# Cross-attention on one core: scalings and weight sums leave VectorE, and the order of sums, moves and steps is set anew

## The chip, the cores and the metric

One Trainium2 chip, one of its cores. The metric is the device time of one execution of the kernel in microseconds, as the median of three runs; beside it one execution was recorded by the profiler. A core has TensorE (matrix products; PE in the profile, its weight loads PEld), VectorE (DVE), ScalarE (ACT), GpSimd (POOL) and SyncE (SP), which here issues nearly all DMA transfers. Each engine works off its own queue of instructions in the order in which the program emits them.

## The reference

All data are float32. There are 8 batch elements of 256 rows and 1024 columns, 32 heads of 32 columns, and 256 context rows per batch element, which serve as keys and as values.

```
mu, var = mean(x), var(x)                       # over the 1024 columns
h = (x - mu) * rsqrt(var + 1e-5) * gamma + beta
Q = split_heads(h @ Wq.T);  K = V = split_heads(ctx)
scores = Q @ K.T / sqrt(32);  scores = where(mask, scores, -inf)
attn = softmax(scores) @ V
out = x + merge_heads(attn) @ Wout.T
```

## The kernel before, in words

**Units of work.** A quad is four heads of one batch element (128 of the 1024 columns), so there are 8 quads for each of the 8 batch elements, 64 in all, numbered from 0. The main loop (line 1006) has one iteration, called slot n below, for each quad. In slot n TensorE computes the scores of quad n+1 (`scores`, line 477), then the values product of quad n-2 (`values`, line 632), and between them and behind them steps of the output projection of an earlier batch element (`product_steps`, line 712) and a part of the query projection of a later one (`make_q`, line 335, or `query_product`, line 436). The other engines do the softmax of quad n+1 (`softmax_parts`, line 505). A block b is the output projection of batch element b; it lies in slots 8(b+1) to 8(b+1)+8, which are counted i = 0 to 8 within the block.

**Softmax of a quad.** For each head j of four and each half s of the 256 rows, VectorE adds the mask and takes the row minimum (line 529), ScalarE takes the exponential and its row sum (line 533). `normalize` (line 538) takes the reciprocal on VectorE and then scales the head's two 128x256 tiles: on GpSimd, unless the table `SCALED_BY` (lines 497 to 503) names ScalarE (A, line 544) or VectorE (V, line 546). This pair of instructions is called a scaling of a quad's head. Then VectorE transposes the head's blocks of 32x32 into `pT` (line 552), ScalarE copies half of that aside to `pc` (line 558), and after the fourth head SP moves pieces between partitions (lines 618 and 622), so that the values product can read them. The score banks in PSUM are four, one for each head: the scores of quad n+2 can only be written once VectorE has read those of quad n+1.

**Projections by Strassen's scheme.** From batch element 2 on the query projection is made of seven products of 512-blocks instead of eight, and so is the output projection of every block (the tables `Q_PRODUCTS` and `PRODUCTS`). That needs sums of weight blocks, made once (`sum_wo` line 177, `sum_wq` line 389; the tables `WO_SUMS` and `WQ_SUMS`, lines 876 to 882, give slot, sum, chunk and engine), and sums of activations for each batch element (`sum_at`, `sum_x`), on GpSimd. The weights' sums for the query are kept in DRAM (`KEEPS`) and come back through the tile `ring`.

**Output steps.** Each block has 28 steps (seven products, four chunks each; a step shows as two instructions in the profile). The tables `FIRST_STEPS` (block 0), `ASIDE_STEPS` (blocks 2 to 5) and `STEPS` (block 1) give, for each slot i of the block, how many steps stand at three places: behind the scores, behind the values product, and behind all the rest of the slot. The bank in which a product accumulates is emptied by VectorE, or ScalarE, at slots fixed in lines 994 to 999 (`take`, `store`, `keep_p1`); what begins in the same bank waits for that.

**Layer norm of a later batch element.** `loads` brings x, `stats` takes mean and variance on VectorE, `norms` normalizes (`ln_norm`, line 245, on ScalarE unless the table `NORM_BY`, line 496, or the call says otherwise), `trans` transposes blocks on VectorE, and `moves` moves 16 pieces between partitions by DMAs on SP (line 331). The slots of these five are given in lines 829 to 858, for batch element 3 and later as distances to the first slot in which the new x is used. Each of them also stands in the order of its engine's queue at that slot.

**Folds.** For batch element 0 the query weights are used as they come; for the later ones each of the 8 chunks is scaled by gamma once (`fold`, line 363), on the engine given by `FOLDED_BY` and at the slots in the list in lines 908 and 935.

**SP's queue.** In each slot SP issues the values of a later quad (line 144), the two moves of line 618, then the loads of the slot (keys, x, residuals, weights of the output projection by `WO_LOADS`, line 210, whose third entry is the slot, or below 0 for the start), the two moves of line 622, and then the moves of x.

Of the kernel before, what the change touches and what calls it, by code (L numbers as in the profile page):

```python
# [59 lines left out]
def xattn_kernel(  # L60
# [149 lines left out]
    WO_LOADS = [[3, 0, -1], [2, 0, 0], [3, 1, -2], [0, 0, 3], [2, 1, -1], [0, 1, -1]]  # L210
# [284 lines left out]
    FOLDED_BY = 'PPVPPPPP'  # L495
    NORM_BY = {(2, 0): nc.vector, (2, 1): nc.gpsimd}
    SCALED_BY = {}
    ENGINES = {"P": nc.gpsimd, "A": nc.scalar, "V": nc.vector}
    for q, j, e in [[63, 2, 'A'], [18, 0, 'V'], [17, 2, 'A'], [16, 2, 'A'], [15, 3, 'A'], [15, 2, 'A'], [15, 0, 'A'],
# [3 lines left out]
        SCALED_BY[q, j] = ENGINES[e]  # L503
# [143 lines left out]
    def copy_at(n):  # L647
# [4 lines left out]
        for r, pv in enumerate(pvs.pop(n)):  # L652
# [22 lines left out]
    FIRST_STEPS = ((0, 0, 0), (0, 4, 2), (0, 2, 3), (0, 1, 1), (0, 3, 1),  # L675
                   (0, 2, 1), (0, 0, 3), (0, 1, 1), (0, 3, 0))
    ASIDE_STEPS = ((0, 0, 0), (0, 6, 0), (0, 2, 0), (0, 4, 0), (0, 4, 2),
                   (0, 0, 1), (0, 1, 4), (0, 0, 0), (0, 4, 0))
# [147 lines left out]
    for b in range(1, B):  # L826
# [3 lines left out]
        elif b == 2:  # L830
            when = dict(
                **{'loads': [0, 1],
         'moves': [5, 5, 5, 5, 5, 5, 6, 6, 6, 6, 6, 7, 7, 7, 7, 7],
         'norms': [3, 3],
# [3 lines left out]
        else:  # L838
            REL = dict(loads=(-13, -12), stats=(-11, -9), norms=(-8, -7), trans=(-7, -6),
                       moves=[-6 + (i + 2) // 6 for i in range(16)])  # L840
            if b == 3:
                REL.update(loads=(-12, -11), stats=(-10, -9))
                REL.update({'loads': [-13, -11],
         'moves': [-6, -6, -5, -5, -5, -5, -5, -5, -5, -4, -4, -4, -4, -3, -3, -3],
         'norms': [-8, -7],
         'stats': [-10, -9],
         'trans': [-6, -6]})
            else:
                REL.update({'loads': [-13, -12],
         'moves': [-6, -6, -6, -6, -6, -6, -6, -5, -5, -5, -4, -4, -4, -4, -4, -4],  # L850
         'norms': [-9, -7],
# [19 lines left out]
        if b % 2 == 0:  # L871
# [351 lines left out]
```

## Time and profile before

| | us |
|---|---|
| median of 3 runs | 583.51 (583.2 to 586.84) |
| profiled execution | 583.09 |
| its span, first to last instruction | 581.3 |
| busy in the span: TensorE / weight loads | 566.2 / 396.1 |
| VectorE / ScalarE / GpSimd | 476.7 / 422.7 / 395.1 |

The share of busy time is not the share of necessary time: matrix instructions are pipelined, and their ends are modelled, so a TensorE that is shown as busy may still be waiting in part. A row of a group reads: line, engine, operation, output and inputs by the program's names, shapes, count, then busy time and the mean time of one, then the idle time of the engine just before them and what ended it. In rows in order of time the first number is the start from the beginning of the span and the second the length; "x2" says that neighbouring instructions are merged. The letters f32 after a shape are the type.

### The profile page before, as it was taken

The numbers are of one execution on the slowest core, as the hardware profiler recorded it, in microseconds if no ns is written. First come the engines' busy times: TensorE is split into PE (matmuls) and PEld (weight loads), VectorE is DVE, ScalarE is ACT, GpSimd is POOL, SyncE is SP. The second block draws the span as 40 slices with busy tenths as digits, with TensorE's granted clock in tenths as the row PEclk, the third lists the DMA queues.
The fourth block names the chain that finished last, engine by engine and source line by source line (L and its number), as shares of the span: only waits on it lengthen the run. The fifth ranks groups of instructions, "written<-read, shape, count | busy, mean of one in ns | idle before, by whom it ended". The sixth has DMA issues, their size and how long they took to land.

```text
span 581.3 us, 20175 instructions
## 1 busy us (share of the span) xinstructions
PE 566.2 (97%) x7258; PEld 396.1 (68%) x7258; DVE 476.7 (82%) x1717; ACT 422.7 (73%) x1465; POOL 395.1 (68%) x628
## 2 busy tenths in 40 slices
PE   8999999799899999999999999999999999999997
PEld 7788885476666776676776777767776777755443
DVE  5999989899897888988889877988978769779823
ACT  4597987678887976787677876788767767769920
POOL 2689996769748665875748866686657667358780
PEclk9999999899999999999999999999999999999999
DMA  8965877657768778887778777777667876446651
GB/s 306 368 173 157 236 202 203 223 172 236 203 198 247 202 193 242 229 223 197 221 209 248 223 214 203 233 220 213 203 160 205 230 198 182 140 133 182 202 164 72
DMA packets 48051, 120.07 MB, mean 207 GB/s; under 512 B 9168, under 2 KB 9936, under 8 KB 47952
## 3 DMA queue, kind: packets, MB, share of 16 engines
q1 hardware_dynamic: 47664, 118.79, 70.4%
q8 instruction: 57, 0.93, 0.7%
q14 instruction: 42, 0.34, 0.2%
q10 hardware_dynamic: 288, 0.01, 0.0%
HBM read 67.38 MB, written 11.53 MB: 136 GB/s over the span
## 4 chain that ended last, share of the span: by engine, by line
PE 66%; DVE 7%; ACT 5%; DMA 2%; issue 1%; POOL 1%; SPq 0%; DVEq 0%
PE po_S L730 16%; PE pq_A L446 16%; PE pv L640 8%; PE sc L485 8%; PE po_A L730 8%; PE pq_S L446 6%; ACT e L533 3%; PE po_end L797 2%; DVE e L529 2%; DVE pT L552 2%; DVE e L546 1%; PE po_last L797 1%; ACT e L544 1%; DMA pT<-pT 1%; POOL e L546 1%
## 5 line engine op out<-in xcount | busy, mean ns | idle before, releaser
L546 POOL TENSOR_SCALAR e<-e,rden 128x256 f32<-128x256 f32 x464 | 215.3, 482 | 135.1 <-DVE rden L540 132.9
L533 ACT ACTIVATE e<-e,mn 128x256 f32<-128x256 f32 x512 | 254.0, 501 | 45.2 <-DVE mn L529 43.5
L552 DVE STREAM_TRANSPOSE pT<-e 128x512 f32<-128x512 f32 x256 | 180.4, 706 | 44.2 <-POOL e L546 33.3
L529 DVE CUSTOM_DVE_ANT_0 e<-sc,mb 128x256 f32<-128x256 f32 x512 | 185.1, 415 | 18.8 <-PE sc L485 18.4
L558 ACT COPY pc<-pT 128x512 f32<-128x512 f32 x128 | 79.0, 617 | 69.9 <-DVE pT L552 40.0
L533 ACT ACTIVATION_READ_ACCUMULATOR e<-e,mn 128x1 f32 x512 | 98.1, 192 | 0.0
L485 PE MATMUL sc<-k,qa 32*128 32x256 f32 x1024 | 74.7, 401 | 1.6 <-DVE qa L467 0.9
L640 PE MATMUL pv<-pT,v 64*32 64x128 f32 x4096 | 74.7, 274 | 0.9 <-DMA pT<-pT 0.8
L730 PE MATMUL po_S<-wo,at 128*128 128x512 f32 x152 | 73.1, 607 | 1.3 <-DVE r L772 0.7
L640 PEld LDWEIGHTS pv<-pT,v 64*32 64x32 f32 x4096 | 57.3, 105 | 24.2 <-issue 15.1
L485 PEld LDWEIGHTS sc<-k,qa 32*128 32x128 f32 x1024 | 46.5, 184 | 36.8 <-issue 13.4
L730 PE MATMUL po_A<-wo,at 128*128 128x512 f32 x128 | 59.6, 606 | 0.2 <-ACT p L738 0.2
L344 PE MATMUL pq<-xnT,wq 128*128 128x256 f32 (+1 forms) x240 | 55.0, 384 | 0.0
L730 PE MATMUL po_S<-wo,s 128*128 128x512 f32 x104 | 50.2, 620 | 3.9 <-DVE r L772 3.5
L446 PEld LDWEIGHTS pq_A<-xnT,wq 128*128 128x128 f32 x416 | 48.2, 192 | 5.1 <-issue 3.9
L344 PEld LDWEIGHTS pq<-xnT,wq 128*128 128x128 f32 x240 | 44.6, 190 | 8.2 <-issue 1.7
L446 PE MATMUL pq_A<-xnT,wq 128*128 128x128 f32 x416 | 49.0, 276 | 0.0
L730 PEld LDWEIGHTS po_S<-wo,at 128*128 128x128 f32 x152 | 26.1, 190 | 25.0 <-issue 22.6
L529 DVE DVE_READ_ACCUMULATOR2_ANT mn<- 128x1 f32 x512 | 42.3, 83 | 0.0
L730 PEld LDWEIGHTS po_A<-wo,at 128*128 128x128 f32 x128 | 22.8, 189 | 25.8 <-issue 24.4
L540 DVE RECIPROCAL rden<-den 128x2 f32<-128x2 f32 x256 | 37.6, 147 | 2.5 <-ACT e L533 1.7
L730 PEld LDWEIGHTS po_S<-wo,s 128*128 128x128 f32 x104 | 19.0, 196 | 23.7 <-issue 19.1
(99 smaller groups left out, 689.1 us busy)
## 6 DMA issues: line engine op xcount, KB each, us to landing
v<-in_kv_dram SPq DMA_DIRECT2D x32, 512.0 KB, 5.1
pT<-pT SPq DMA_DIRECT2D x128, 128.0 KB, 2.6
pT<-pc SPq DMA_DIRECT2D x128, 128.0 KB, 3.8
ring<-kept_T SPq DMA_DIRECT2D x22, 512.0 KB, 5.9
k<-in_kv_dram SPq DMA_DIRECT2D x32, 256.0 KB, 3.8
x<-in_x_dram SPq DMA_DIRECT2D x14, 512.0 KB, 5.1
r<-in_x_dram SPq DMA_DIRECT2D x28, 256.0 KB, 4.7
out_dram<-r SPq DMA_DIRECT2D x28, 256.0 KB, 2.7
```

The costliest lines, as they stand in the source:

```text
L344: nc.tensor.matmul(pqs[n], wq[:, o, c, :], xnTs[b](c), start=(c == 0), stop=(c == NC - 1),)
L446: nc.tensor.matmul(pqs[b][:, o, :], w[:, c], x_[:, c], start=begins and o + c == 0, stop=c == NK - 1, skip_group_check=True,)
L485: nc.tensor.matmul(scs[n][j][:, s, :], qa[r, n % NQ, ts(s, P)], ks[n - n % 2][r, n % 2, :], start=True, stop=True,)
L529: nc.vector.tensor_tensor_reduce(out=e[:, s, :], in0=pss[j][:, s, :], in1=mbs[n // NQ], scale=1.0, scalar=NO_SCORE, op0=ALU.add, op1=ALU.m ...
L533: nc.scalar.activation(e[:, s, :], e[:, s, :], AF.Exp, bias=mn[:, s : s + 1], scale=-1.0, accum_out=den[:, s : s + 1],)
L540: nc.vector.reciprocal(rden, dens[j])
L546: engine.tensor_scalar(es[j][:, s, :], es[j][:, s, :], rden[:, s : s + 1], 1.0, ALU.mult, ALU.mult,)
L552: nc.vector.transpose(pT[:, :, :, j, :, :].rearrange("p a i s k -> p (a i) s k"), es[j].rearrange("p s (b t) -> p b s t", t=K),)
L558: nc.scalar.copy(pc[:, :, ts(j, 2)], pT[:, 1, :, ts(j, 2)])
L640: nc.tensor.matmul(pvs[n][r][j * HD : (j + 1) * HD], vs[n - n % 2][ts(r, 2 * K), n % 2, i, ts(j, HD)], pT[ts(r, 2 * K), :, i, j, :, :], st ...
L730: nc.tensor.matmul(po, operand(b, name)[:, c], wo[:, which, c], start=begins and c == 0, stop=c == NK - 1, skip_group_check=not begins,)
L797: nc.tensor.matmul(po, end_operand(name)[:, c], wo[:, which, c, cols], start=c in begins, stop=True, skip_group_check=True,)
```

## The change

It alters tables and two engine assignments; no computation is added or left out.

- Scaling: the seven pairs on VectorE (quads 1, 5, 10 twice, 12 twice, 18) go to GpSimd or ScalarE. ScalarE scales 20 pairs, all in quads 3 to 16, instead of 17; in quad 10 these are heads 0, 1 and 2. GpSimd scales 236 pairs instead of 232.
- Weight sums: the three query sums on VectorE go to GpSimd, and the slots of many sums are new.
- Folds: all on GpSimd, at new slots (two before slot 0 instead of one).
- Normalization: the second half of batch element 1 goes from GpSimd to VectorE, the second half of element 2 from GpSimd to ScalarE.
- Output steps of block 0 and blocks 2 to 5 are spread over their slots in another way; the same 28 for each.
- Loads, moves, norms and transpositions of batch elements 2 and later are at other slots in part, and so are some loads of output weights and the keeping of sums. In the diff the first table with `moves` is that of batch element 2, the second that of element 3, the third that of elements 4 to 7.

```diff
-    WO_LOADS = [[3, 0, -1], [2, 0, 0], [3, 1, -2], [0, 0, 3], [2, 1, -1], [0, 1, -1]]
+    WO_LOADS = [[3, 0, -1], [0, 0, 3], [0, 1, 1], [3, 1, -1], [2, 0, 2], [2, 1, 2]]
...
-    FOLDED_BY = 'PPVPPPPP'
-    NORM_BY = {(2, 0): nc.vector, (2, 1): nc.gpsimd}
+    FOLDED_BY = 'PPPPPPPP'
+    NORM_BY = {(2, 0): nc.vector}
...
-    for q, j, e in [[63, 2, 'A'], [18, 0, 'V'], [17, 2, 'A'], [16, 2, 'A'], [15, 3, 'A'], [15, 2, 'A'], [15, 0, 'A'],
-         [14, 3, 'A'], [13, 3, 'A'], [12, 3, 'V'], [12, 2, 'A'], [12, 1, 'V'], [11, 3, 'A'], [11, 2, 'A'],
-         [10, 3, 'V'], [10, 0, 'V'], [9, 3, 'A'], [8, 3, 'A'], [6, 3, 'A'], [6, 2, 'A'], [5, 3, 'A'],
-         [5, 2, 'A'], [5, 0, 'V'], [1, 0, 'V']]:
+    for q, j, e in [[3, 3, 'A'], [4, 3, 'A'], [5, 3, 'A'], [6, 2, 'A'], [6, 3, 'A'], [8, 3, 'A'], [10, 0, 'A'],
+         [10, 1, 'A'], [10, 2, 'A'], [11, 1, 'A'], [11, 2, 'A'], [11, 3, 'A'], [12, 2, 'A'], [13, 2, 'A'],
+         [13, 3, 'A'], [14, 3, 'A'], [15, 0, 'A'], [15, 2, 'A'], [15, 3, 'A'], [16, 2, 'A']]:
...
-    FIRST_STEPS = ((0, 0, 0), (0, 4, 2), (0, 2, 3), (0, 1, 1), (0, 3, 1),
-                   (0, 2, 1), (0, 0, 3), (0, 1, 1), (0, 3, 0))
-    ASIDE_STEPS = ((0, 0, 0), (0, 6, 0), (0, 2, 0), (0, 4, 0), (0, 4, 2),
-                   (0, 0, 1), (0, 1, 4), (0, 0, 0), (0, 4, 0))
+    FIRST_STEPS = ((0, 0, 0), (0, 5, 0), (0, 3, 0), (0, 4, 3), (0, 1, 0),
+                   (0, 3, 0), (0, 1, 3), (0, 1, 1), (0, 3, 0))
+    ASIDE_STEPS = ((0, 0, 0), (0, 4, 4), (0, 0, 4), (0, 0, 1), (0, 3, 1),
+                   (0, 0, 0), (0, 3, 4), (0, 0, 0), (0, 4, 0))
...
-                **{'loads': [0, 1],
-         'moves': [5, 5, 5, 5, 5, 5, 6, 6, 6, 6, 6, 7, 7, 7, 7, 7],
-         'norms': [3, 3],
+                **{'loads': [0, 0],
+         'moves': [5, 5, 5, 5, 5, 6, 6, 6, 6, 6, 6, 6, 7, 7, 7, 7],
+         'norms': [2, 3],
...
-                REL.update({'loads': [-13, -11],
-         'moves': [-6, -6, -5, -5, -5, -5, -5, -5, -5, -4, -4, -4, -4, -3, -3, -3],
-         'norms': [-8, -7],
+                REL.update({'loads': [-13, -10],
+         'moves': [-6, -6, -6, -6, -5, -5, -5, -5, -4, -4, -4, -4, -4, -4, -4, -4],
+         'norms': [-9, -7],
          'stats': [-10, -9],
-         'trans': [-6, -6]})
+         'trans': [-7, -6]})
...
-         'moves': [-6, -6, -6, -6, -6, -6, -6, -5, -5, -5, -4, -4, -4, -4, -4, -4],
-         'norms': [-9, -7],
+         'moves': [-6, -6, -6, -6, -6, -6, -6, -5, -5, -4, -4, -4, -4, -4, -4, -4],
+         'norms': [-9, -8],
...
-    WO_SUMS = [[6, 4, 1, 'P'], [2, 5, 1, 'P'], [5, 4, 0, 'P'], [3, 5, 0, 'P'], [5, 5, 2, 'P'], [11, 6, 1, 'P'],
-         [13, 3, 1, 'P'], [6, 5, 3, 'P'], [11, 6, 2, 'P'], [9, 4, 2, 'P'], [12, 6, 3, 'P'], [11, 6, 0, 'P'],
-         [10, 4, 3, 'P'], [14, 3, 3, 'P'], [13, 3, 0, 'P'], [12, 3, 2, 'P']]
-    WQ_SUMS = [[11, 'T2', 0, 'P'], [10, 'T3', 2, 'P'], [8, 'T3', 1, 'V'], [6, 'T1', 2, 'P'], [7, 'T1', 1, 'P'],
-         [5, 'T1', 0, 'P'], [10, 'T3', 3, 'P'], [7, 'T1', 3, 'P'], [12, 'T2', 2, 'P'], [14, 'T4', 3, 'P'],
-         [8, 'T3', 0, 'V'], [14, 'T4', 1, 'P'], [12, 'T2', 3, 'P'], [14, 'T4', 2, 'P'], [10, 'T2', 1, 'V'],
+    WO_SUMS = [[5, 4, 1, 'P'], [13, 3, 1, 'P'], [3, 5, 1, 'P'], [3, 5, 0, 'P'], [4, 5, 2, 'P'], [10, 6, 1, 'P'],
+         [9, 6, 2, 'P'], [6, 5, 3, 'P'], [5, 4, 0, 'P'], [6, 4, 2, 'P'], [10, 4, 3, 'P'], [14, 3, 3, 'P'],
+         [11, 6, 0, 'P'], [12, 6, 3, 'P'], [13, 3, 0, 'P'], [12, 3, 2, 'P']]
+    WQ_SUMS = [[8, 'T1', 2, 'P'], [11, 'T2', 0, 'P'], [10, 'T3', 2, 'P'], [10, 'T3', 3, 'P'], [8, 'T3', 1, 'P'],
+         [4, 'T1', 0, 'P'], [7, 'T1', 1, 'P'], [7, 'T1', 3, 'P'], [8, 'T3', 0, 'P'], [14, 'T4', 1, 'P'],
+         [12, 'T2', 3, 'P'], [14, 'T4', 2, 'P'], [12, 'T2', 2, 'P'], [14, 'T4', 3, 'P'], [10, 'T2', 1, 'P'],
          [13, 'T4', 0, 'P']]
...
-    KEEPS = [[9, 'T1', 0], [10, 'T1', 1], [9, 'T3', 0], [11, 'T3', 1], [8, 'B11', 0], [10, 'B11', 1]]
+    KEEPS = [[10, 'T1', 0], [10, 'T1', 1], [9, 'T3', 0], [11, 'T3', 1], [7, 'B11', 0], [12, 'B11', 1]]
...
-        foldat = [1, 0, -1, 2, 4, 4, 4, 7]
+        foldat = [-1, -1, 0, 2, 2, 4, 5, 7]
...
-    ln_norm(1, 1, nc.gpsimd)
+    ln_norm(1, 1, nc.vector)
```

More of the change, by code (lines that the diff above doesn't have):

```diff
@@ L934, in xattn_kernel @@
             (begun if n % 2 else ended)[halves[n]] = n
-    for o, n in enumerate([1, 0, -1, 2, 4, 4, 4, 7]):
+    for o, n in enumerate([-1, -1, 0, 2, 2, 4, 5, 7]):
         FOLDS_AT.setdefault(n, []).append(o)
```

## The prediction

> **What bounds the kernel now.** First the page's head, then busy time in three stretches, cut where TensorE begins the scores of quads 1, 10, 19 and 63 (a quad is four heads of one batch element; slot n of the loop computes the scores of quad n+1). Columns: width, then busy time (instructions) of PE, PEld, DVE, ACT, POOL, the granted clock, DMA share, GB/s.
>
> ```profile
> span 581.3 us, 20175 instructions
> ```
> ```profile
> 22.53:90.01 67.48, 66.64 (x817) 53.46 (x816) 61.77 (x236) 58.24 (x203) 62.23 (x79) 1.00 0.72 206
> 90.01:178.13 88.12, 80.84 (x1015) 53.54 (x1014) 78.16 (x251) 66.56 (x224) 63.48 (x79) 0.98 0.70 207
> 178.13:545.40 367.27, 366.44 (x4961) 255.87 (x4961) 306.70 (x1145) 277.80 (x976) 246.05 (x431) 1.00 0.73 205
> ```
>
> The profiled execution took 583.09 us, 1.8 more than its span; the median of the three runs is 583.51. From 178 to 545 us TensorE idles 0.83 us: that stretch can only lose. From 90 to 178 it idles 7.3 us, and being busy there is not being quick. What it must do shows in the chain of waits, in a slot where nothing is waited for (start, length, work):
>
> ```profile
> 253.01 1.08 PE sc L485 x16
> 254.08 1.08 PE pv L640 x64
> 255.17 3.63 PE po_S L730 x8
> 258.80 3.57 PE pq_S L446 x32
> ```
>
> Slots 9 to 17 hold nine times scores and values (9 x 2.16 = 19.4), seven query products (7 x 3.57 = 25.0) and 35 output steps of two instructions each (28 of block 0, 7 of block 1: 70 x 3.63/8 = 31.8): 76.2 us against 88.12. So **11.9 us** are to be had here. The largest piece, on PE:
>
> ```profile
> 110.19 4.48 PE L730 MATMUL po_S<-wo,s 128*128 128x512 f32 x6 [3.54 <-DVE r L772]
> ...
> 124.41 2.84 PE L730 MATMUL po_S<-wo,at 128*128 128x512 f32 x6
> ```
>
> It waits 3.54 us for VectorE to empty the output bank, and then six instructions take 4.48 instead of 2.84: 1.64 more, at the lowered clock behind the 0.98. (The Trainium skill, page "TensorE: Matmul & The Clock Gate", section "What's actually happening", says that one idle window of about 3.4 us halves the clock. This row agrees; by the rule both parts go together or not at all.)
>
> VectorE is late because of these rows (DVE; the first row of quads 10, 11, 12, 13 is an L529), with GpSimd at the same time:
>
> ```profile
> 93.25 0.41 DVE L529 CUSTOM_DVE_ANT_0 e<-sc,mb 128x256 f32<-128x256 f32 x1
> 95.50 2.63 DVE L546 TENSOR_SCALAR e<-e,rden 128x256 f32<-128x256 f32 x2
> 100.77 2.73 DVE L546 TENSOR_SCALAR e<-e,rden 128x256 f32<-128x256 f32 x2
> 106.23 0.41 DVE L529 CUSTOM_DVE_ANT_0 e<-sc,mb 128x256 f32<-128x256 f32 x1
> 114.11 1.60 DVE L395 TENSOR_TENSOR wq<-wq 128x512 f32<-128x512 f32 x1
> 115.76 0.42 DVE L529 CUSTOM_DVE_ANT_0 e<-sc,mb 128x256 f32<-128x256 f32 x1
> 119.38 2.62 DVE L546 TENSOR_SCALAR e<-e,rden 128x256 f32<-128x256 f32 x2
> 123.35 2.44 DVE L546 TENSOR_SCALAR e<-e,rden 128x256 f32<-128x256 f32 x2
> 126.94 0.38 DVE L529 CUSTOM_DVE_ANT_0 e<-sc,mb 128x256 f32<-128x256 f32 x1
> ```
> ```profile
> 95.38 1.27 POOL L434 TENSOR_TENSOR sx<-xnT 128x512 f32<-128x512 f32 x1 [3.20 <-DMA xnT<-xe]
> ```
>
> Quad 10 takes VectorE 12.98 us, of which 5.36 scale; quad 12 takes 11.18, of which 5.06 scale. A VectorE scaling lasts as long as the GpSimd sum beside it.
>
> **The change part by part.** Prices, from the groups by line and form (busy us, mean ns):
>
> ```profile
> L546 POOL TENSOR_SCALAR e<-e,rden 128x256 f32<-128x256 f32 x464 | 215.3, 482 | 135.1 <-DVE rden L540 132.9 <-DVE mv L233 0.3
> L533 ACT ACTIVATE e<-e,mn 128x256 f32<-128x256 f32 x512 | 254.0, 501 | 45.2 <-DVE mn L529 43.5 <-POOL rstd L238 1.4
> L558 ACT COPY pc<-pT 128x512 f32<-128x512 f32 x128 | 79.0, 617 | 69.9 <-DVE pT L552 40.0 <-DVE rden L540 28.7
> L544 ACT ACTIVATE e<-e,rden 128x256 f32<-128x256 f32 x34 | 15.4, 500 | 2.2 <-DVE rden L540 2.1
> L315 DVE STREAM_TRANSPOSE xe<-x 128x1024 f32<-128x1024 f32 x12 | 14.4, 1206 | 0.0
> L546 DVE TENSOR_SCALAR e<-e,rden 128x256 f32<-128x256 f32 x14 | 12.9, 965 | 0.2
> L183 POOL TENSOR_TENSOR wo<-wo 128x512 f32<-128x512 f32 x16 | 20.4, 1289 | 0.0
> L395 POOL TENSOR_TENSOR wq<-wq 128x512 f32<-128x512 f32 x9 | 11.9, 1343 | 0.0
> L256 POOL TENSOR_SCALAR x<-x,mv,rstd 128x1024 f32<-128x1024 f32 x2 | 8.5, 4262 | 0.1
> L395 DVE TENSOR_TENSOR wq<-wq 128x512 f32<-128x512 f32 x3 | 2.9, 978 | 0.0
> L365 DVE TENSOR_TENSOR wq<-wq,gs 128x1024 f32<-128x1024 f32 x1 | 1.3, 1311 | 0.0
> L256 DVE TENSOR_SCALAR x<-x,mv,rstd 128x1024 f32<-128x1024 f32 x4 | 3.2, 797 | 0.1
> ```
>
> Whole kernel: VectorE loses 14 scalings (12.9), three sums (2.9) and a fold (1.3) and gains one normalization (0.8): -16.3. ScalarE gains 6 scalings (6 x 0.45 = 2.7) and one normalization of x. GpSimd gains 8 scalings (3.9), three sums (4.0) and the fold, and loses two normalizations (8.5): about even. (The Trainium skill, page "GPSIMD Engine Reference", section "4.1 Engine selection", would keep sums of two inputs on VectorE, GpSimd being about twice as slow. The rows show 1343 against 978 ns, and it speaks against this part, for GpSimd pays 4.0 where VectorE saves 2.9.)
>
> Stretch 22 to 90 us. TensorE loses one idle spell here:
>
> ```profile
> 28.22 0.98 PE L306 MATMUL px<-ring,x 128*128 128x128 f32 x7 [0.76 <-POOL x L256]
> ```
>
> That normalization goes from GpSimd (4.26) to VectorE (0.80), which drops a fold of 1.31 at the same place: the wait goes, **-0.8**, and nothing else is late, as VectorE also drops a scaling in quad 1. The output weights of B22 now load in slot 2 instead of at the start and in slot 0, and the sums that need them stand in slot 3: GpSimd may wait for them, and quad 5's scaling behind it. I take 2 us of delay on GpSimd there and nothing on TensorE, since its queue then holds at most four pairs and two or three sums or folds a slot and catches up; at worst 1 us.
>
> Stretch 90 to 178. GpSimd's queue behind quad 9 becomes the tight place. In the new order it does four pairs of scalings (3.9), three 128x512 sums of activations (3 x 1.29) and three sums of query weights (4.0), some 12 us, where now it has 6.8. Its activation sums wait for the moves of x:
>
> ```profile
> 89.35 4.39 SPq L331 DMA_DIRECT2D xnT<-xe  x5
> ```
>
> Four moves instead of five stand there (-0.9), and the slot comes 1.2 to 1.8 us sooner (VectorE without its two sums and lag): the sums start near 92.7, not 95.38. Two of these and three weight sums take until 99.3, and only then comes the one scaling of quad 10 left to GpSimd (head 3), done at 100.3; ScalarE does heads 0 to 2 meanwhile (8 x 0.50 + 3 x 0.91 = 6.7). What VectorE has left then, at most the 2.7 us that stand between 103.50 and 106.23 now, puts quad 11 near 102.6, 3.6 sooner. Of the 5.4 of scaling in quad 10 and the 3.2 of lag at its start (93.25 - 90.01), 5.0 go back to GpSimd.
> Quad 11: ScalarE's 4.0 of exponentials, three scalings (2.7) and two copies (1.2) make 7.9, so quad 12 starts at 110.5 (now 115.76). There VectorE scales nothing, but GpSimd comes late: four 128x512 sums and two small operations stand ahead of quad 11's one scaling (done near 107.3), then five sums of weights and one of activations (7.9, to 115.2), then three pairs (2.9, to 118.1), a transposition of the scores and one of x: quad 13 at 119.9 (now 126.94), **-7.0**. TensorE's 3.54 wait goes, with the 1.64 behind it, because by the new steps the S2 product stands one slot after the emptying and not right behind it.
> Quads 13 to 18: quad 18's VectorE scaling goes (1.9), and one x transposition of two leaves quad 13 (0.7 of its 1.2 counted): -2.6. GpSimd has 0.9 less in quads 10 to 16 together (one pair and one output-weight sum less, one query-weight sum more), counted as nothing. Against this TensorE meets weights summed just in time (the output's T2 in slot 11, the query's T2 in slot 13): 1.5 us, between 0 and two sums each, 5.3. Together **-8.1** of the 11.9.
>
> Stretch 178 to 545. The idle time is one wait on PE. The name it carries is a DMA's of another quad; the values of quad 48 themselves were issued late on SP, and a load of values takes 5.1 us in the median (last row, the page's DMA issues):
>
> ```profile
> 451.00 1.25 PE L640 MATMUL pv<-pT,v 64*32 64x128 f32 x64 [0.83 <-DMA pT<-pT]
> ```
> ```profile
> 444.54 0.43 SPq L144 DMA_DIRECT2D v<-in_kv_dram  x1
> ```
> ```profile
> v<-in_kv_dram SPq DMA_DIRECT2D x32, 512.0 KB, 5.1
> ```
>
> 444.54 + 0.43 + 5.1 = 450.1: about when TensorE goes on. New steps in blocks 2 to 5 put two more output steps into a block's slot 1 and S2 into its slot 2, so these values are needed 1.8 us later, against one move more ahead in the queue (4.39/5 = 0.9): **-0.8**. S2 comes there right behind VectorE's emptying:
>
> ```profile
> 313.20 1.15 PE L485 MATMUL sc<-k,qa 32*128 32x256 f32 x16
> ...
> 316.28 0.41 DVE L529 CUSTOM_DVE_ANT_0 e<-sc,mb 128x256 f32<-128x256 f32 x1
> ...
> 319.09 0.69 DVE L768 TENSOR_TENSOR r<-po_A,r 128x512 f32<-128x512 f32 x1
> ```
>
> That is slot 2 of a block. TensorE would get to S2 2.16 + 3.57 after 313.20, at 318.9, VectorE is done at 319.8: 0.9 late. But TensorE's slot start moves back by the two added steps (1.8) and VectorE's doesn't, so I take 0; at most 4 x 0.9 = 3.6. End: the last quad's third scaling goes from ScalarE to GpSimd: between -0.9 (a pair less on ScalarE) and +1.0 (a pair more on GpSimd), taken as 0, as either stands beside the other.
> Sum: 583.1 - 0.8 - 8.1 - 0.8 = **573.4**.
>
> **The rivals.**
> 1. GpSimd's pile takes more: the moves of x land as late as now (95.38), quad 10's last scaling ends at 103.0, where VectorE's own ends now (103.50). Then quad 10 gives nothing and 3.6 of the gain goes; with the 1 us bounded in the first stretch, 573.4 + 3.6 + 1.0 = 578. For it: 3.20 us of waiting there today. Against: one move less.
> 2. TensorE alone paces: all 11.9 come: 583.1 - 0.8 - 11.9 - 0.8 = 569.6. For it: the 367 us after, at 0.83 idle. Against: quads 10 to 12 have 9 to 12 us on GpSimd or ScalarE, and slots of 7 to 12 on TensorE.
> 3. Slower: GpSimd paces quads 9 to 16 and keeps its idle time (88.12 - 63.48), as its in-order queue waits for the same divisors, moves and loads. Then its 5.0 more behind quad 9 less 0.9 count in full, and TensorE twice waits as it did at 110.19, with 1.64 behind each wait: 583.1 - 0.8 + 4.1 + 3.3 = 589.7. It decides once quad 10's last scaling ends after 107.
> 4. The change doesn't do what it says, because the scaling costs ScalarE what VectorE saves: nothing moves but the first wait, 582.3. Against: 0.91 a pair there, 2.4 to 2.7 here.
>
> **How the numbers follow.** Forecast 0.56 (570.5 to 576.5), rival 1 0.20, rival 2 0.12, rival 3 0.08, rival 4 0.04. The range 569 to 580.5 holds the first three and leaves out 0.12. One per cent, about what a measurement tells from no change, is 5.8: below 577.7 lie the forecast, rival 2 and some of rival 1: 0.76; above 589.3 rival 3: 0.08; the rest 0.16.
>
> **What would show it.** The stretch from the scores of quad 10 to those of quad 19 at 79 to 81 us instead of 88.12; no L546 (one line up by then) on DVE; quad 10 still over 11 us on VectorE, ended by a GpSimd scaling; no wait over 2 us of TensorE on VectorE near 110; 178 to 545 at the same length or 0.8 less. I am wrong if that last stretch grows, or if GpSimd's waits for moves or weights land in quads 11 to 16.

## The result, and the profile after

The changed kernel takes 581.55 us (median of 16 runs) beside 584.0 us for the kernel before: a ratio of 0.9937, 95% interval 0.9912 to 0.9961. A second measurement gave 579.89 beside 584.32, a ratio of 0.9912 (0.9885 to 0.994). The change gains 0.6 to 0.9%; the forecast was 1.7%. The profiled execution took 581.48 us. The ratios, here and below, leave out two runs that took over 1.5% longer than the fastest of their kernel (590.63 and 583.98 us, named with their kernels), and the medians keep them.

First the page's head, then the stretches of the prediction, cut at the same places (TensorE begins the scores of quads 1, 10, 19 and 63; columns as before).

```profile
span 579.7 us, 20189 instructions
```
```profile
22.11:90.02 67.91, 66.11 (x817) 53.33 (x816) 61.59 (x234) 60.43 (x206) 55.70 (x81) 1.00 0.72 199
90.02:174.66 84.64, 80.25 (x1015) 54.20 (x1014) 65.08 (x238) 68.94 (x231) 68.95 (x89) 0.96 0.73 215
174.66:543.65 368.99, 367.33 (x4961) 255.63 (x4960) 306.22 (x1142) 278.95 (x975) 244.90 (x428) 1.00 0.74 205
```

| stretch | before | forecast | after |
|---|---|---|---|
| up to quad 1 | 22.53 | 22.53 | 22.11 |
| quads 1 to 10 | 67.48 | -0.8 | 67.91 (+0.4) |
| quads 10 to 19 | 88.12 | -8.1 | 84.64 (-3.5) |
| quads 19 to 63 | 367.27 | -0.8 | 368.99 (+1.7) |
| behind (581.3 - 545.40; 579.7 - 543.65) | 35.9 | 0 | 36.05 (+0.15) |

VectorE's load went as told: 78.16 us of work became 65.08 in the middle stretch, and no scaling is left on it. TensorE did not get what VectorE gave. It is busy 80.25 of 84.64 us, but at a mean clock of 0.96 (0.98 before), and its waits have a new name. PE in order of time; in brackets the idle time before the row and what ended it:

```profile
68.38 1.25 PE L639 MATMUL pv<-pT,v 64*32 64x128 f32 x64 [1.78 <-DMA pT<-pT]
...
101.40 2.08 PE L639 MATMUL pv<-pT,v 64*32 64x128 f32 x64 [3.58 <-DMA pT<-pT]
103.41 4.95 PE L729 MATMUL po_A<-wo,at 128*128 128x512 f32 x6
...
176.75 1.25 PE L639 MATMUL pv<-pT,v 64*32 64x128 f32 x64 [0.94 <-DMA v<-in_kv_dram]
```

Each of them is the first values product of a pair of quads (4, 8 and 16), which needs a load of values; a row may name another transfer that ended earlier. The values of quad 8 landed at 101.16, 0.24 us before the product began. The 3.54 us for which TensorE waited for VectorE at 110.19 are gone, as forecast; 3.58 us of waiting for the values of quad 8 stand in their place, again with slow matmuls behind them (six instructions 4.95 us instead of 2.84, the values product 2.08 instead of 1.16). Of the 3.58, TensorE coming sooner than before (97.82 instead of 99.93) makes 2.11 and the later landing (101.16 instead of 98.63) 2.53, less what there was to spare.

VectorE and GpSimd at the same time:

```profile
91.31 0.39 DVE L528 CUSTOM_DVE_ANT_0 e<-sc,mb 128x256 f32<-128x256 f32 x1
...
103.83 0.71 DVE L551 STREAM_TRANSPOSE pT<-e 128x512 f32<-128x512 f32 x1 [3.88 <-POOL e L545]
105.52 1.29 DVE L230 BATCH_NORM_STATS2 st<-x 128x6 f32<-128x512 f32 x2 [0.98 <-DMA x<-in_x_dram]
...
107.16 0.41 DVE L528 CUSTOM_DVE_ANT_0 e<-sc,mb 128x256 f32<-128x256 f32 x1
...
115.74 0.39 DVE L528 CUSTOM_DVE_ANT_0 e<-sc,mb 128x256 f32<-128x256 f32 x1
...
124.97 0.42 DVE L528 CUSTOM_DVE_ANT_0 e<-sc,mb 128x256 f32<-128x256 f32 x1 [0.77 <-PE sc L485]
```
```profile
96.58 1.27 POOL L434 TENSOR_TENSOR sx<-xnT 128x512 f32<-128x512 f32 x1 [4.16 <-DMA xnT<-xe]
...
100.39 2.49 POOL L395 TENSOR_TENSOR wq<-wq 128x512 f32<-128x512 f32 x2
102.86 0.94 POOL L545 TENSOR_SCALAR e<-e,rden 128x256 f32<-128x256 f32 x2
```

Quad 10 now takes VectorE 15.8 us (91.31 to 107.16) instead of 13.0, though 5.4 us of scaling are gone from it. GpSimd starts its sums of x at 96.58, when the moves of x have landed, works through the weight sums, and scales head 3 of quad 10 at 102.86, done at 103.80; behind that VectorE waits again, for half a load of x.

All three late things, the values, the moves of x and the load of x, are issued by SP. Its queue after, and then the rows that answer to it before (start, time to issue, count):

```profile
49.70 0.97 SPq L173 DMA_DIRECT2D wo<-in_woT_dram  x2
...
57.21 1.13 SPq L173 DMA_DIRECT2D wo<-in_woT_dram  x2
...
59.75 0.59 SPq L144 DMA_DIRECT2D v<-in_kv_dram  x1
...
78.32 4.30 SPq L331 DMA_DIRECT2D xnT<-xe  x7
...
91.33 3.72 SPq L331 DMA_DIRECT2D xnT<-xe  x4
95.09 0.58 SPq L404 DMA_DIRECT2D kept_B<-wq  x1
95.72 0.49 SPq L144 DMA_DIRECT2D v<-in_kv_dram  x1
...
98.92 0.49 SPq L130 DMA_DIRECT2D x<-in_x_dram  x1
...
158.96 6.09 SPq L331 DMA_DIRECT2D xnT<-xe  x8
...
169.87 0.50 SPq L144 DMA_DIRECT2D v<-in_kv_dram  x1
```
```profile
56.92 1.12 SPq L173 DMA_DIRECT2D wo<-in_woT_dram  x2
...
59.28 0.58 SPq L144 DMA_DIRECT2D v<-in_kv_dram  x1
...
77.63 3.04 SPq L331 DMA_DIRECT2D xnT<-xe  x5
...
87.07 0.57 SPq L130 DMA_DIRECT2D x<-in_x_dram  x1
...
93.79 0.58 SPq L144 DMA_DIRECT2D v<-in_kv_dram  x1
```

Two loads of output weights that stand in slot 2 now are issued at 49.70; the two right ahead of the values of quad 4 (57.21) stood there before too (56.92). Slot 6 got two moves more (7 for 5), and the last moves start at 91.33 and not at 89.35 although they are one fewer. A store of kept weights moved ahead of the values of quad 8, which are issued at 95.72 instead of 93.79; and the half of x went from slot 7 to slot 8 and is issued at 98.92 instead of 87.07. Before the change TensorE's values had little to spare: the loads of quads 6, 8 and 24 landed 0.87, 1.30 and 0.14 us ahead of their use, and that of quad 48 was waited for.

### The profile page after: what moved, and what is told of

Same layout as the page of the kernel before. It is cut to its first block, busy times and chain, and to the rows that moved or that the text cites. A ratio compares the mean times of both kernels' runs of the same rounds, so it can differ in the third digit from the quotient of the medians.

```text
span 579.7 us, 20189 instructions
## 1 busy us (share of the span) xinstructions
PE 566.6 (98%) x7258; PEld 397.1 (68%) x7258; DVE 463.2 (80%) x1700; ACT 427.7 (74%) x1472; POOL 395.7 (68%) x639
## 4 chain that ended last, share of the span: by engine, by line
PE 65%; ACT 9%; DVE 9%; DMA 8%; POOL 4%; issue 3%; SPq 1%; DVEq 0%; POOLq 0%; ACTq 0%
PE po_S L729 15%; PE pq_A L446 15%; PE pv L639 8%; PE sc L485 8%; PE po_A L729 7%; PE pq_S L446 6%; ACT e L532 6%; DVE e L528 3%; POOL e L545 3%; PE po_end L796 2%; DVE pT L551 2%; DMA x<-in_x_dram 2%; ACT e L543 2%; DMA pT<-pT 2%; DVE st L230 1%
## 5 line engine op out<-in xcount | busy, mean ns | idle before, releaser
L545 POOL TENSOR_SCALAR e<-e,rden 128x256 f32<-128x256 f32 x472 | 218.9, 482 | 136.8 <-DVE rden L539 134.7
L532 ACT ACTIVATION_READ_ACCUMULATOR e<-e,mn 128x1 f32 x512 | 100.2, 196 | 0.0
L729 PE MATMUL po_S<-wo,s 128*128 128x512 f32 x104 | 47.9, 598 | 0.0
L729 PEld LDWEIGHTS po_A<-wo,at 128*128 128x128 f32 x128 | 24.0, 196 | 28.1 <-issue 26.9
L652 ACT COPY at<-pv 128x128 f32<-128x128 f32 x128 | 26.3, 255 | 9.1 <-PE pv L639 9.1
```

Of the source, the lines that this page charges most:

```text
L532: nc.scalar.activation(e[:, s, :], e[:, s, :], AF.Exp, bias=mn[:, s : s + 1], scale=-1.0, accum_out=den[:, s : s + 1],)
L545: engine.tensor_scalar(es[j][:, s, :], es[j][:, s, :], rden[:, s : s + 1], 1.0, ALU.mult, ALU.mult,)
L652: nc.scalar.copy(ats[b, k][:, c, :, ts(r, 2), :], pv.rearrange("p a s k -> p s a k"))
L729: nc.tensor.matmul(po, operand(b, name)[:, c], wo[:, which, c], start=begins and c == 0, stop=c == NK - 1, skip_group_check=not begins,)
```

## The experiments

The first theory: the bound moved from VectorE to SP's queue, and late loads of values, x and moves eat the gain. The second: GpSimd's pile of sums behind quad 9 holds VectorE, wherever the loads stand. The third: the new output steps cost time. "Slot" and "quad" are used as in the prediction. Ratios are to the kernel before on the same chip.

| kernel | median us | ratio (95%) | quad 8 | quad 10 | quad 12 | quad 19 | span |
|---|---|---|---|---|---|---|---|
| before | 584.0 | | 74.9 | 90.0 | 114.6 | 178.1 | 581.3 |
| changed | 581.55 | 0.9937 (0.9912-0.9961) | 74.9 | 90.0 | 111.9 | 174.7 | 579.7 |
| changed, again | 579.89 | 0.9912 (0.9885-0.994) | 75.0 | 90.1 | 110.0 | 173.8 | 579.3 |
| engines alone | 581.31 | 0.9926 (0.9895-0.9957) | 73.4 | 92.8 | 111.9 | 176.1 | 581.8 |
| old queue | 577.96 | 0.9875 (0.9827-0.9924) | 73.0 | 88.1 | 107.1 | 172.3 | 575.3 |
| values early | 581.77 | 0.993 (0.9896-0.9965) | 72.8 | 87.9 | 106.1 | 173.2 | 576.2 |
| old steps | 583.4 | 0.9951 (0.9921-0.9981) | 74.6 | 89.9 | 114.1 | 173.0 | 579.4 |
| head 3 on ScalarE | 579.12 | 0.9897 (0.9849-0.9945) | 73.8 | 88.9 | 111.5 | 173.7 | 576.6 |
| values, head 3, x | 580.12 | 0.9908 (0.9869-0.9948) | 73.1 | 88.2 | 103.4 | 173.6 | 576.7 |
| old queue, values | 582.16 | 0.9946 (0.9916-0.9975) | 73.1 | 88.1 | 107.0 | 175.1 | 578.7 |
| old queue, values, head 3 | 580.69 | 0.9912 (0.9877-0.9947) | 73.0 | 88.0 | 103.2 | 172.6 | 576.4 |
| old queue, head 3 | 576.48 | 0.985 (0.9805-0.9896) | 73.0 | 89.0 | 104.9 | 170.5 | 573.2 |
| old output-weight loads | 579.2 | 0.9918 (0.9889-0.9946) | 74.0 | 89.1 | 108.3 | 172.4 | 576.1 |
| old x | 578.74 | 0.9896 (0.9855-0.9938) | 73.5 | 93.2 | 108.3 | 175.3 | 577.4 |
| old moves | 579.53 | 0.9898 (0.987-0.9926) | 74.3 | 90.2 | 109.1 | 173.8 | 577.1 |

The columns of quads give where TensorE begins the scores of that quad in the one profiled execution. Neighbouring ratios overlap, so the waits in the traces carry more than the order of the medians; but each trace is one execution.

**Engines alone**: the kernel before, with the table of scalings, the two tables below and the normalization of x of block 1 as in the change, and the three sums of query weights on VectorE given to GpSimd in their old slots.

```diff
-    FOLDED_BY = 'PPVPPPPP'
-    NORM_BY = {(2, 0): nc.vector, (2, 1): nc.gpsimd}
+    FOLDED_BY = 'PPPPPPPP'
+    NORM_BY = {(2, 0): nc.vector}
...
-         [8, 'T3', 0, 'V'], [14, 'T4', 1, 'P'], [12, 'T2', 3, 'P'], [14, 'T4', 2, 'P'], [10, 'T2', 1, 'V'],
+         [8, 'T3', 0, 'P'], [14, 'T4', 1, 'P'], [12, 'T2', 3, 'P'], [14, 'T4', 2, 'P'], [10, 'T2', 1, 'P'],
```

> The kernel before with the change's engines alone: its scalings, folds, weight sums and normalization stand on the engines of the change; its output steps, its order of loads, moves and stores and its slots of sums are those of before. Theory 1 (the new order on the SP queue brings values, moves of x and an x load late, and eats the gain): the engines alone bring more than the whole change, 577 us, 575 to 579.5; the values of quads 4 and 8 wait less than 0.5 us on TensorE. Theory 2 (GpSimd's pile behind quad 9 holds VectorE, wherever the loads stand): quad 10 still takes over 14 us on VectorE and the time is 580 to 584. Theory 3 (the new output steps cost time): at most 579, below the changed kernel, whatever stands on the SP queue.

581.31: no theory's number but the second's, and not for its reason. (The profiled execution, 583.58, was the second slowest of twelve.) Quad 10 takes VectorE 11.1 us, not over 14, and the values of quads 4 and 8 are not waited for; it is those of quad 6 that come late, for 2.48 us:

```profile
84.59 1.26 PE L639 MATMUL pv<-pT,v 64*32 64x128 f32 x64 [2.48 <-DMA v<-in_kv_dram]
```

These values are the ones with 0.87 us to spare before. A quicker TensorE comes for them sooner and finds them missing in this execution. The engines alone gain about what the whole change gains.

**Old queue**: the changed kernel, with the old slots of what SP issues: output-weight loads, x of blocks 2 and up (with its normalizations and transpositions) and keeps.

```diff
-    WO_LOADS = [[3, 0, -1], [0, 0, 3], [0, 1, 1], [3, 1, -1], [2, 0, 2], [2, 1, 2]]
+    WO_LOADS = [[3, 0, -1], [2, 0, 0], [3, 1, -2], [0, 0, 3], [2, 1, -1], [0, 1, -1]]
...
-         'moves': [5, 5, 5, 5, 5, 6, 6, 6, 6, 6, 6, 6, 7, 7, 7, 7],
+         'moves': [5, 5, 5, 5, 5, 5, 6, 6, 6, 6, 6, 7, 7, 7, 7, 7],
...
-    KEEPS = [[10, 'T1', 0], [10, 'T1', 1], [9, 'T3', 0], [11, 'T3', 1], [7, 'B11', 0], [12, 'B11', 1]]
+    KEEPS = [[9, 'T1', 0], [10, 'T1', 1], [9, 'T3', 0], [11, 'T3', 1], [8, 'B11', 0], [10, 'B11', 1]]
```

> The changed kernel with the order of before on the SP queue: the slots of output-weight loads, x loads, moves of x and keeps (and with them those of the statistics' normalizations and transpositions of x) are those of before; engines, sums' slots and output steps stay changed. Theory 1: 577 us, 575 to 579.5; the waits for values of quads 4 and 8 (1.78 and 3.58 us in the changed kernel) shrink below 1 us each and the scores of quad 19 begin before 173. Theory 2: the wait of GpSimd for the moves of x stays over 3 us, quad 10 stays over 14 us on VectorE, 580.5 to 583. Theory 3: same as the changed kernel, 580.5 to 582.5.

577.96, within the first theory's range and outside the others'. The wait of quad 4 is gone, that of quad 8 is 2.19 instead of 3.58 (below 1 was expected), and quad 19's scores begin at 172.3. GpSimd's wait for moves stays (3.92) and so does the length of quad 10 on VectorE, 14.5 us, as the second theory has it: both things are there. The ratio's interval still overlaps those of the changed kernel (0.9875 beside 0.9937 and 0.9912), so that the traces say more here than the time.

```profile
98.05 2.08 PE L639 MATMUL pv<-pT,v 64*32 64x128 f32 x64 [2.19 <-DMA pT<-pT]
```

**Values early**: each load of values one slot sooner.

```diff
-        ahead = [partial(load_v, n)] if n > 1 and n % 2 == 0 else []
+        ahead = [partial(load_v, n + 1)] if n % 2 and n + 1 < N else []
```

> The changed kernel with each load of values one slot sooner on the SP queue, ahead of the moves and stores of that slot; nothing else differs. Theory 1: no wait of TensorE for values over 0.5 us in quads 4, 8, 16 and 24; scores of quad 8 begin 1.8 us sooner (73.1), those of quad 12 about 2 us sooner (VectorE is the next bound there), 577 us, 575 to 579. Theory 2: quad 12 begins where it does (111.9) and the time falls by at most the 1.8 of quad 7, of which the pile takes some back: 580 to 581.5. Theory 3: 580.5 to 582.

The waits for values go: they land 5 us and more ahead. The profiled execution took 577.95, as the first theory has it, but it is the quickest of twelve; the median is 581.77, so the expectation is missed. The trace shows one price. The values now stand ahead of the moves of x, which reach GpSimd 7.96 us after quad 10's scores (95.81 - 87.85) instead of 6.56, and VectorE becomes the wait at quad 12:

```profile
95.81 1.28 POOL L434 TENSOR_TENSOR sx<-xnT 128x512 f32<-128x512 f32 x1 [4.68 <-DMA xnT<-xe]
```
```profile
106.10 4.20 PE L485 MATMUL sc<-k,qa 32*128 32x256 f32 x16 [3.02 <-DVE mn L528]
```

The slower executions have no trace; what they wait for is open.

**Head 3 on ScalarE**: the one scaling of quad 10 that stands behind GpSimd's pile is taken out.

```diff
-         [10, 1, 'A'], [10, 2, 'A'], [11, 1, 'A'], [11, 2, 'A'], [11, 3, 'A'], [12, 2, 'A'], [13, 2, 'A'],
+         [10, 1, 'A'], [10, 2, 'A'], [10, 3, 'A'], [11, 1, 'A'], [11, 2, 'A'], [11, 3, 'A'], [12, 2, 'A'], [13, 2, 'A'],
```

> The changed kernel with the one scaling of quad 10 that GpSimd does behind its pile (head 3, done at 103.8) moved to ScalarE, as heads 0 to 2; nothing else differs. Theory 1: VectorE starts quad 11 one to four us sooner, but TensorE begins quad 12 within 1 us of 111.9, since the values of quad 8 land late; 580.5 to 582. Theory 2: quad 10 takes 10 to 12.5 us on VectorE instead of 15.8, quad 12's scores begin by 109.5, 577 to 579.5. Theory 3: 580.5 to 582.5.

579.12, within the second theory's range, but the trace is not as it says. Quad 12 begins at 111.5, as the first theory has it, with TensorE waiting 4.26 us for the values of quad 8; and quad 10 on VectorE does not get shorter: it takes 16.5 us. The scaling is done by 99.4, and then VectorE stands 4.87 us for the half of x that the change loads one slot later:

```profile
105.01 1.29 DVE L230 BATCH_NORM_STATS2 st<-x 128x6 f32<-128x512 f32 x2 [4.87 <-DMA x<-in_x_dram]
```

So there were three late things at quads 10 to 12, one behind the other's cover.

**Old steps**: the output steps of before (both tables) in the changed kernel.

```diff
-    FIRST_STEPS = ((0, 0, 0), (0, 5, 0), (0, 3, 0), (0, 4, 3), (0, 1, 0),
+    FIRST_STEPS = ((0, 0, 0), (0, 4, 2), (0, 2, 3), (0, 1, 1), (0, 3, 1),
...
-    ASIDE_STEPS = ((0, 0, 0), (0, 4, 4), (0, 0, 4), (0, 0, 1), (0, 3, 1),
+    ASIDE_STEPS = ((0, 0, 0), (0, 6, 0), (0, 2, 0), (0, 4, 0), (0, 4, 2),
```

> The changed kernel with the output steps of before in block 0 and in blocks 1 to 5 (the two tables of steps); engines, sums and the order on the SP queue stay changed. Theory 3 (the new steps cost time): faster than the changed kernel, 579 or less. Theory 1 (the SP queue): the values of quads 4 and 8 land as late as in the changed kernel and TensorE waits for them; in blocks 2 to 5 values are needed 1.8 us sooner and are waited for once or twice more; 581 to 585, and TensorE waits again over 2 us for VectorE to empty the output bank near quad 11.

583.4 (580.49 to 590.63), the first theory's range; the third falls. The values of quads 24 and 40 are waited for, 1.24 and 1.40 us, as expected. The wait for the emptied bank near quad 11 comes back as 1.59 us, not over 2:

```profile
111.34 2.84 PE L729 MATMUL po_S<-wo,s 128*128 128x512 f32 x6 [1.59 <-DVE r L771]
```

From quad 10 to quad 19, where the forecast gave the new steps the 3.54 us of waiting and 1.64 behind it, the old ones cost nothing in this execution: 83.2 us, beside 84.6 and 83.7 in the two executions of the changed kernel. They cost from quad 19 to quad 63: 370.7 us, beside 369.0 and 368.5.

**Values, head 3 and x**: both edits above, and the half of x of block 3 back in slot 7 (`'loads': [-13, -10]` to `[-13, -11]`).

> The changed kernel with three things at once: each load of values one slot sooner on the SP queue, head 3 of quad 10 scaled by ScalarE, and the second half of x of block 3 loaded in slot 7 instead of slot 8. In the changed kernel each of them holds quads 10 to 12 alone when the others are gone (the values of quad 8 land at 101.2, GpSimd scales head 3 at 103.8, the x load lands near 105). Theory 1, in this form (late loads, in parallel with GpSimd's pile, so that nothing short of all three shows the gain): quad 10 takes 11 to 12.5 us on VectorE, scores of quad 12 begin by 105.5 instead of 111.9, those of quad 19 by 170.5 instead of 174.7; 575 us, 573 to 577.5. Theory 2 (GpSimd's pile paces whatever stands on SP): the pile is only handed on to quads 11 and 12, quad 19 begins after 172.5; 578 to 581.

580.12. Quad 10 takes 11.5 us on VectorE and quad 12's scores begin at 103.4, as the first theory has it; the time is the second's, for there the gain ends. GpSimd waits 6.07 us for the moves of x; behind them stand the sums; behind the sums a small operation on the statistics of block 3; and for that ScalarE waits with the normalization that the change moved ahead to slot 9, and with it all exponentials of quad 11:

```profile
97.55 1.28 POOL L434 TENSOR_TENSOR sx<-xnT 128x512 f32<-128x512 f32 x1 [6.07 <-DMA xnT<-xe]
```
```profile
105.36 1.24 ACT L251 ACTIVATE x<-x,shift,rstd 128x1024 f32<-128x1024 f32 x1 [4.29 <-POOL shift L248]
```
```profile
108.51 2.07 PE L485 MATMUL sc<-k,qa 32*128 32x256 f32 x10 [3.69 <-DVE mn L528]
```

The pile is handed on, as the second theory said, and what feeds it is late by the first.

**Old queue, values early; and the same with head 3 on ScalarE.** Two kernels, each made of edits above.

> The changed kernel with the order of before on the SP queue (as in the run with the old queue) and each load of values one slot sooner. Theory 1: the 2.2 us wait for the values of quad 8 and the small ones go, quad 10's last scaling by GpSimd then holds (VectorE's quad 10 still 14 us or more): 576 us, 574.5 to 577.5, 1 to 3 us below the old queue alone. If earlier values only push the moves of x later, as happened with the new queue: the same as the old queue alone or slower, 577.5 to 580.

> The changed kernel with the order of before on the SP queue, each load of values one slot sooner, and head 3 of quad 10 scaled by ScalarE. Theory 1 (loads and the pile in parallel): quad 10 takes at most 12.5 us on VectorE, scores of quad 12 begin by 104.5, those of quad 19 by 169.5; 574 us, 572 to 576. Theory 2 (the pile is handed on): quad 19 begins after 171.5, 576 to 578.5.

582.16 and 580.69, both slower than any case had it (580 and 578.5 at most). In the first kernel the traces go the way of the other case: earlier values push the moves of x back (GpSimd waits 6.17 us for them, 3.92 with the old queue alone). In the second quad 10 takes 11.5 us and quad 12's scores begin at 103.2, but quad 19 begins at 172.6, as the pile is handed on: TensorE waits 2.30 us for an output bank that VectorE empties late. Why the medians lie above the old queue's by so much, the one trace of each does not show.

```profile
96.67 1.27 POOL L434 TENSOR_TENSOR sx<-xnT 128x512 f32<-128x512 f32 x1 [6.17 <-DMA xnT<-xe]
```
```profile
108.30 6.76 PE L729 MATMUL po_S<-wo,s 128*128 128x512 f32 x8 [2.30 <-DVE r L771]
```

**Old queue and head 3 on ScalarE**, values where they were.

> The changed kernel with the order of before on the SP queue and head 3 of quad 10 scaled by ScalarE; values load where they did. Theory 1: with x early, nothing but the scaling holds quad 10, which ends by 101.5 on VectorE (103.8 with the old queue alone); TensorE still waits 2 us for the values of quad 8, so quad 12's scores come by 106.6 and the gain over the old queue alone is at most 1.5 us: 576 to 578.5. If the pile of GpSimd is only handed on: quad 11 takes over 10 us on VectorE (8.6 with the old queue alone), quad 12 starts there no sooner than 111.5, and the time is that of the old queue alone, 577 to 579.

576.48, ratio 0.985 (0.9805 to 0.9896): quicker than the kernel before and than the changed one. Five of its six runs took 574.96 to 577.26, and the sixth 583.98; the changed kernel beside it on the chip took 577.26 to 581.63. VectorE begins quad 11 at 101.59 (expected by 101.5) and TensorE waits 0.55 for quad 8's values, so that quad 12's scores come at 104.9, earlier than the 106.6 I gave as the bound. No wait of TensorE is over 1 us, and the granted clock is 1.00:

```profile
89.00:170.53 81.53, 77.98 (x1016) 52.79 (x1015) 62.89 (x231) 68.63 (x230) 64.22 (x78) 1.00 0.77 225
```
```profile
94.04 1.27 POOL L434 TENSOR_TENSOR sx<-xnT 128x512 f32<-128x512 f32 x1 [3.43 <-DMA xnT<-xe]
```
```profile
101.59 0.41 DVE L528 CUSTOM_DVE_ANT_0 e<-sc,mb 128x256 f32<-128x256 f32 x1
...
110.45 0.38 DVE L528 CUSTOM_DVE_ANT_0 e<-sc,mb 128x256 f32<-128x256 f32 x1
...
119.07 0.42 DVE L528 CUSTOM_DVE_ANT_0 e<-sc,mb 128x256 f32<-128x256 f32 x1 [0.22 <-PE sc L485]
```
```profile
97.34 1.26 PE L639 MATMUL pv<-pT,v 64*32 64x128 f32 x64 [0.55 <-DMA pT<-pT]
```

**The parts of the old queue.** On the same chip as the last: the changed kernel again, with the old slots of output-weight loads alone (`WO_LOADS` as above), and with those of x of blocks 2 and 3 and of the keeps.

> The changed kernel itself once more, for a second profiled execution and a comparison on one chip with the three beside it. If the lengthening by 1.7 us of the stretch from quad 19 to quad 63 belongs to the change: 368.5 to 369.5 again. If it is the landing of single loads in that execution (in the run with head 3 of quad 10 on ScalarE the same code took 367.1): 366.5 to 368. The time 580 to 583; the waits for values of quads 4 and 8 stay over 0.8 and over 2.5 us.

> The changed kernel with the slots of the output-weight loads of before alone (two of them no longer stand in slot 2). Theory 1: the wait for the values of quad 4 (1.78) goes, since two loads of 512 KB no longer stand right ahead of them, and quad 8's scores begin by 73.5 instead of 74.9; all behind is held by the same loads and moves at quads 9 to 11, shifted: 579.5 to 581.5. If these loads don't matter: 581 to 582.5 and a wait over 1 us at quad 4.

> The changed kernel with the slots of before for x of blocks 2 and 3 (loads, normalizations, transpositions, moves) and for the keeps; output-weight loads and blocks 4 to 7 stay changed. Theory 1: x of block 2 lands by 95 instead of 96.6 and the second half of x of block 3 early; VectorE begins quad 11 by 105, TensorE quad 12 by 109; the wait at quad 4 stays; 578 to 580. If it is the pile's length and not where x lands: VectorE begins quad 11 after 106.5 and the time is 580.5 to 582.5.

The changed kernel again: waits for values of quads 4, 8 and 16 of 2.02, 2.92 and 1.55 us, and 368.45 us from quad 19 to quad 63, at the border of my two cases. The wait for quad 16's values is in both executions; SP issues eight moves of x in one slot there (the row at 158.96; four and three before), and with the old queue those values landed 1.19 us ahead. So part of the 1.7 us seems to belong to the change; that it is the eight moves is not shown, for with the old output-weight loads and with the old moves, which leave them, quad 16's values are not waited for.

With the old output-weight loads, 579.2: quad 4's values are still waited for, 0.56 us, and quad 8 begins at 74.0, not by 73.5; the expected time was 579.5 to 581.5. The two loads right ahead of these values stay where they are in that kernel, so what I expected of it rested on a misreading. With the old slots of x and keeps, 578.74, as expected, but the wait at quad 4 does not stay: the values land 1.17 us ahead, with all the changed output-weight loads in place. And VectorE begins quad 11 at 106.75, not by 105: the values of quad 6 came 2.78 us late in that execution and shifted everything behind, and quad 10 itself takes 12.4 us on VectorE instead of 15.8. The medians lie 0.7 and 1.15 us below the changed kernel's beside them (579.89), within the spread of its runs, so that the shares of the parts are not told apart.

```profile
84.94 1.26 PE L639 MATMUL pv<-pT,v 64*32 64x128 f32 x64 [2.78 <-DMA v<-in_kv_dram]
```

**Old moves**: of all that, only the moves of x of block 2.

```diff
-         'moves': [5, 5, 5, 5, 5, 6, 6, 6, 6, 6, 6, 6, 7, 7, 7, 7],
+         'moves': [5, 5, 5, 5, 5, 5, 6, 6, 6, 6, 6, 7, 7, 7, 7, 7],
```

> The changed kernel with the slots of before for the moves of x of block 2 alone (6, 5 and 5 moves in slots 5, 6 and 7 instead of 5, 7 and 4). If the two moves that the change puts into slot 6 are what keeps the queue back: GpSimd's first sum of x starts within 5.5 us of quad 10's scores (6.6 in the changed kernel), quad 10's last scaling ends 1 us sooner, and the time is 578 to 580. If they are not, and the loads of output weights and values in front keep the queue back: the sum starts 6 us or more after quad 10's scores and the time is that of the changed kernel, 579.5 to 582.

579.53, which lies in both ranges. The sum starts 4.94 us after quad 10's scores (95.17 - 90.23; 6.56 and 5.67 in the two executions of the changed kernel) and head 3 is scaled by 102.4 instead of 103.8, as expected if the two moves keep the queue back. But with the old output-weight loads, where the two moves stay in slot 6, it starts 5.12 us after, so one execution of each does not show that it is the moves. VectorE doesn't get it: it stands 2.36 us for the half of x.

```profile
95.17 1.26 POOL L434 TENSOR_TENSOR sx<-xnT 128x512 f32<-128x512 f32 x1 [3.32 <-DMA xnT<-xe]
```
```profile
105.48 1.29 DVE L230 BATCH_NORM_STATS2 st<-x 128x6 f32<-128x512 f32 x2 [2.36 <-DMA x<-in_x_dram]
```

## Why the prediction was wrong

**What held.** VectorE lost what was counted, GpSimd and ScalarE took it at about the prices of the rows (a scaling on ScalarE 509 ns, a sum of query weights on GpSimd 1276). Quad 10 is over 11 us and was released by a GpSimd scaling; no wait of TensorE for VectorE over 2 us is left near 110; the waits at 28.22 and 451.00 are gone. From quad 13 to quad 19 VectorE gained 2.7 us (54.6 before, 51.9 after; 52.7 in the second execution), forecast 2.6.

**The step that failed** is "the sums start near 92.7" in the part on quads 10 to 13. I took one move fewer in slot 7 (-0.9) and a slot that comes 1.2 to 1.8 us sooner, and did not count the two moves that the change puts into slot 6, ahead in the same queue. The sums start at 96.58, 1.2 us later than before (95.80 in the second execution), and in no kernel here before 94.04. The fewer moves did save 0.8: from the first one's issue to the sums it is 5.25 us instead of 6.03. The earlier slot did not come for SP: TensorE begins quad 10 at 90.02, as before (90.01), and with the five old moves put back the last ones start at 89.42 (before 89.35). With two moves more in slot 6 the last moves start at 91.33 and 90.76 in the two executions of the changed kernel, but at 88.99 with the old output-weight loads, where those two moves stay and quad 10 begins only 0.9 sooner. How much of the delay comes from the two moves is therefore open. From 96.58 the step's own lengths give the rest: the last scaling done at 103.8 instead of 100.3, quad 11 at 107.16 instead of 102.6, quad 12 at 115.74 instead of 110.5, quad 13 at 124.97 instead of 119.9. The miss is 4.6 at quad 11 and still 5.1 at quad 13; what I worked out between them, 7.9 and 9.4, came to 8.6 and 9.2. Where the old queue brings the half of x in time and head 3 is off the pile, the same quads begin at 101.59, 110.45 and 119.07, and the stretch takes 81.5 us against the 80.0 of the forecast.

**What the sum left out** is the other end of that queue. The text asked of each moved load who waits for its own data (sums for weights, bounded at 2 us on GpSimd: 1.40 measured), and up to quad 19 never who stands behind it. The values of quad 4 come 1.78 us late, which takes back the first stretch (2.0 us ahead by quad 4, where 0.8 was forecast, and level again at quad 8); the values of quad 8 come 3.58 late, with about 3 us of slow matmuls (2.08 - 1.16 and 4.95 - 2.84); the half of x 0.98 late behind the pile. These lie beside the late pile, not on top of it, so that no single one, taken away, shows its full length. The Trainium skill's page "DMA: Bandwidth & Descriptors", section "Queues, rings and completion order", says that a DMA engine takes the descriptors of one issuing queue in order; the trace before agrees as far as landings show it: the eight transfers that SP issued from 56.92 to 65.25 landed in that order, from 61.48 to 68.97.

What makes the values of quad 4 late is open in part. TensorE would have taken them at 66.6 instead of 68.47, and the load takes longer: issued at 59.28 it landed at 65.97 before, issued at 59.86 at 68.24 in the second execution of the changed kernel. The two loads of 512 KB right ahead of it are the same in both. In the five traces with the changed slots of output weights and of the loads of x, and the values in their place, the wait is 0.84 to 2.02 us; with the old output-weight loads it is 0.56, with the old x and keeps nothing, with the old queue nothing. Either part put back takes most of it, in one execution each.

**Rival 1 is what came**, at 0.20: its condition, moves of x as late as now and the last scaling at 103.0, was met with 96.58 and 103.8 (95.80 and 103.0 in the second execution). Its price of 578 is 3.5 short of 581.55, and it had no waits for values in it. Rival 4's 582.3 is the nearest number, and its reason is not what came: VectorE's work fell by 13 us in the middle stretch, TensorE's wait for it at 110.19 went, and the stretch got 3.5 us shorter. Rival 2 fell with the waits, rival 3's point of 107 was not reached.

**Smaller terms.** The 1.5 us for weights summed just in time measured nothing in this execution (0.40 in the second). The -0.8 at quad 48 came, and 0.94 and 0.53 us of waiting for the values of quads 16 and 24 came with it; I had named a longer last stretch as a sign of error. The end moved by 0.15, forecast 0. The 5.2 us that the forecast gave the new steps (the wait of 3.54 and 1.64 behind it) do not show as theirs: with the old steps 1.59 of waiting comes back, and the stretch from quad 10 to quad 19 does not get longer.

## What to carry to other kernels

When a change moves loads or moves between slots, go through the issuing queue row by row and give everything that stands behind them its slack, landing against use; here loads with 0.1 to 1.3 us to spare were waited for once TensorE came sooner. Where several late things end in the same wait, undo them together as well as one by one: the parts alone showed 1 to 2 us or nothing here, within the spread, and the old queue with one scaling moved showed 1.5% against 0.6 to 0.9%.

## What the runs showed of the hardware

A wait of TensorE of 2.2 us was enough for slow matmuls behind it: with the old queue the values product behind the 2.19 us took 2.08 instead of 1.16 us and the clock of the stretch was 0.98; with head 3 moved as well, the wait was 0.55, the product took 1.26 and the clock was 1.00. The other traces agree. Behind the first 20 us they hold 14 waits of 2.19 to 4.26 us, and after each the granted clock is at 0.50 within 2 us; they hold 15 waits of 1.03 to 2.02 us, and after none of them does it fall. The Trainium skill's page "TensorE: Matmul & The Clock Gate", section "What's actually happening", speaks of an idle window of about 3.4 us. Nine of the 14 waits, 2.19 to 3.02 us, are shorter than that by themselves. But the scores ahead of the 2.19 use 32 rows of the array and not 128, and from the last full product to the values product it is 3.27 us there (94.78 to 98.05), and 3.10 us at the wait of 2.02. Whether such narrow products count as idle, no run here tells.

Loads of the same size differ much in how long they take, in one execution and between two: behind the start, the values' loads took 3.6 to 8.4 us in the second execution of the changed kernel, and the wait at quad 8 was 3.58 in one of its executions and 2.92 in the other. With so little slack this may be what shows in the time: the changed kernel's 16 runs spread over 578.1 to 583.7, the six with the old queue over 577.1 to 578.8. Moving all values ahead did not narrow it (578.0 to 584.9), and why not is open.
